# An LSTM with a binary FFN behind it: seven products for one block of 256 columns a quarter, and seven for two blocks of 512 a quarter

## Chip, cores and metric

The kernel runs on one core of a Trainium2 chip. The metric is the device time of one execution in microseconds (us); where several runs are given, it is their median.

## The reference

`x` is 32 sequences of 64 steps and 256 features. An LSTM with 256 units runs over it, and its hidden states go through a feed-forward network (FFN) of three layers whose weights are +1 or -1; the result is added to `x`.

```python
def step(carry, xw_t):                       # 64 steps, xW = x @ Wx + b
    prev_h, prev_c = carry
    a = xw_t + prev_h @ Wh                   # 32 x 1024
    i, f, o = sigmoid of the first three quarters of a
    g = jnp.tanh(a[:, 3 * Hd:])
    next_c = f * prev_c + i * g
    next_h = o * jnp.tanh(next_c)
    ...
h = jnp.concatenate([h, -h], axis=-1)        # all 2048 rows of hidden states
h = jax.nn.relu(s0 * _conn_dense(k0, h)) * 2     # 512 -> 1024
h = jax.nn.relu(s1 * _conn_dense(k1, h)) * 2     # 1024 -> 1024
h = s2 * _conn_dense(k2, h)                      # 1024 -> 256
return x + h
```

`_conn_dense` multiplies by a matrix that is 1.0 where its boolean kernel is true and -1.0 elsewhere.

## The kernel before

**Blocks.** The 64 steps are four blocks of 16 steps. A block gives the FFN 16 x 32 = 512 columns. In the FFN every activation is split into a high and a low part (`h` and `l`, fp32r tiles), and both are multiplied, so a product of one 128 x 128 piece of weights is two matmuls of 512 columns. Layer 0 of a block is 8 chunks of 4 matmuls (L594), the second layer ("layer 1", L620) 8 chunks of 16, layer 2 (L607) 32 matmuls: 192 in all (`ffn_block`). A chunk is evicted from PSUM by `evict` (L365): ScalarE writes relu to `h` (L368), VectorE writes the rest to `l` (L369).

**Steps.** A loop over the 64 steps issues, for each step: the products of h with Wh on TensorE (`gates_from_h`, L308: 32 matmul instructions in the trace), then the cell (`cell_step`): `sig`, `cand`, `sig` on ScalarE (L325 to L327), `kept`, `new` and `c` on VectorE (L329 to L333), `th` on ScalarE (L335), `h` and its transpose into `hist` on VectorE (L337, L342), and two ScalarE copies that put the next step's x part into the gate banks (L319, L320). Then comes a quota of other matmuls from a generator: products of x with Wx up to step 20 (`X_STEPS`, L63), FFN work from step 21 on. The quota is spread evenly:

```python
total_ffn = (NB - 1) * (4 * FC0 + 2 * FC0 * FC1 + 4 * FC1)
goal = (t + 1) * total_x // X_STEPS if t < X_STEPS else (t + 1 - X_STEPS) * total_ffn // (T - X_STEPS)
```

Here `total_ffn` is 576, three blocks. After the quota a step may issue one small chore: the split of four steps' h into `hhi` and `hlo` (`split_h`, L361, L362), a piece of weights, a sum of weight quarters (`make_sum`, L418), an output step (`output`, L372). The order of the program is kept on every engine (`manual_schedule`), so each engine has one queue and the matmuls of step t stand between the gates of t and those of t + 1.

**The last block** has its inputs only after the last step. `last_block` runs behind the loop. Its second layer is done in seven products instead of eight: weights and activations are cut into quarters (512 rows by 512 weights, and 512 rows by half of the block's columns, 256), and sums and differences of quarters are multiplied. The four tables of weight sums `s1` to `s4` are made in the steps, the sums and differences of activations (`differ`, `split`, L443, L449, L450) behind them, all on VectorE and ScalarE. A product is 32 matmuls of 256 columns (L459), so the seven are 224. Layer 2 (L564) is 64 matmuls of 256 columns, whose output has time as rows; `finish` scales it, adds x and stores it. The PSUM banks are four `pf`, two `po` and the two gate banks.

**Pools.** The x parts, the weight sums and the split quarters lie in `gpool` (28 buffers of 2 KB a partition), other activations in `apool` (24 buffers).

Of the kernel before, what the change touches and what calls it, by code (L numbers as in the profile page):

```python
# [43 lines left out]
def lstm_ffn(ctx: ExitStack, tc: tile.TileContext, x, cond, wx_d, wh_d, b_d, k0_d, k1_d, k2_d, s0_d, s1_d, s2_d, out):  # L44
# [29 lines left out]
    gpool = ctx.enter_context(tc.tile_pool(name="xg", bufs=28))  # L74
    apool = ctx.enter_context(tc.tile_pool(name="act", bufs=24))
# [28 lines left out]
    wh = const.tile([P, 2, G], F32, name="wh")  # L104
    wx = wpool.tile([P, 2, G], F32, tag="wx", name="wx")
    w0 = const.tile([P, 2, F0], F32R, name="w0")
# [154 lines left out]
    def evict_x(p, t):  # L261
        xg[t] = gpool.tile([P, 2, 4 * HQ], F32, tag="xg", name=f"xg{t}")
        b = bias.rearrange("p g j -> p (g j)").unsqueeze(1).to_broadcast([P, 2, 4 * HQ])
        load[0] += 1
        nc.vector.tensor_tensor(xg[t], p.rearrange("p t g j -> p t (g j)"), b, ALU.add)  # L265
# [132 lines left out]
    K2, F2, CB = FC0 // 2, F1 // 2, TB // 2  # L398
    sums = {}

    def make_sum(s, k):
# [3 lines left out]
        if s == 4:  # L405
            if k == 0:

                sums[s] = wpool.tile([P, K2, F2], F32R, tag="wx", name="s4")
            t = sums[s][:, k]
        else:  # L410
            t = gpool.tile([P, F2], F32R, tag="xg", name=f"s{s}_{k}")
# [9 lines left out]
    def parts(pool, tag, name):  # L421
        return [pool.tile([P, 2, CB], F32R, tag=tag, name=f"{name}{s}") for s in "hl"]

    def last_block(b):

        hi, lo = hparts.pop(b)
        full, b11, b2, t, a1 = [], {}, {}, {}, {}
        t2 = hpool.tile([P, K2, CB], F32, tag="hlo", name="t2")
        u = hpool.tile([P, 2, 2, CB], F32, tag="hhi", name="u")

        def quarter(i, k):

            return {1: full[k][:, 0], 2: t2[:, k], 3: full[k][:, 1], 4: full[K2 + k][:, 0]}[i]

        def differ(i, k):

            in0, in1 = {
                1: (full[k][:, 1], full[k][:, 0]),
                2: (full[K2 + k][:, 1], full[k][:, 0]),
                3: (full[K2 + k][:, 1], full[k][:, 1]),  # L440
                4: (full[K2 + k][:, 0], t2[:, k]),
            }[i]
            nc.vector.tensor_tensor(quarter(i, k), in0, in1, ALU.subtract)  # L443

        def split(i, k):
            if k % 2 == 0:
                t[i, k // 2] = parts(gpool, "xg", f"t{i}_{k}")
            h, l = (a[:, k % 2] for a in t[i, k // 2])
            nc.scalar.copy(h, quarter(i, k))  # L449
            nc.vector.tensor_tensor(l, quarter(i, k), h, ALU.subtract)  # L450

        def side(i):
            return lambda k, n: t[i, k // 2][n][:, k % 2]

        def product(bank, pair, a, b, first, last):
            for i in range(2):
                for k in range(K2):
                    for n in range(2):
                        nc.tensor.matmul(  # L459
                            bank[pair][:, i],  # L460
                            a(k)[:, ts(2 * pair + i, P)],
                            b(k, n),
                            start=first and i == 0 and k == 0 and n == 0,
                            stop=last and k == K2 - 1 and n == 1,
                            skip_group_check=True,
                        )

        def bank(name):
            return [ps_f.tile([P, 2, CB], F32, tag="pf", name=f"{name}{pair}") for pair in range(2)]

        def take(rows, half, pair, p):

            h, l = parts(apool, "act", f"c{rows}{half}_{pair}")
            nc.scalar.activation(h, p, AF.Relu)
            nc.vector.scalar_tensor_tensor(l, p, 0.0, h, ALU.max, ALU.subtract)
            for i in range(2):
                a1[rows * K2 + 2 * pair + i, half] = h[:, i], l[:, i]

        def take_sum(rows, half, pair, p, c):
            nc.vector.tensor_tensor(c, p, c, ALU.add)  # L480
            take(rows, half, pair, c)

        for m in range(FC0):
            p = ps_f.tile([P, TB], F32, tag="pf", name=f"p0_{b}_{m}")
            for n, (k, a) in enumerate(((0, hi), (0, lo), (1, hi), (1, lo))):
                nc.tensor.matmul(p, w0[:, k, ts(m, P)], a[:, k, :], start=(n == 0), stop=(n == 3))  # L486
            f = act([P, 2, CB], F32, f"f_{m}")
            full.append(f)
            nc.scalar.activation(f.rearrange("p c n -> p (c n)"), p, AF.Relu)
            if m < K2:  # L490
                if m % 2 == 0:
                    b11[m // 2] = parts(apool, "act", f"b11_{m}")
                h, l = (t[:, m % 2] for t in b11[m // 2])
                f = f[:, 0]
            else:
                b2[m - K2] = h, l = parts(apool, "act", f"b2_{m}")
            nc.scalar.copy(h, f)
            nc.vector.tensor_tensor(l, f, h, ALU.subtract)
            if m > K2:
                for i in (1, 2):  # L500
                    differ(i, m - K2 - 1)
            yield

        res = [xpool.tile([P, 2, D], F32, tag="x", name=f"res{half}") for half in range(2)]
        for i in range(NQ):
            nc.sync.dma_start(out=res[i // 2][:, i % 2], in_=x_in[:, ts(b * NQ + i, SH)])
        for i in (1, 2):
            differ(i, K2 - 1)


        x = bank("x")
        q = [g.rearrange("p (i n) -> p i n", i=2) for g in gate_banks]

        for pair in range(2):
            product(x, pair, lambda k: w1[:, k, :F2], lambda k, n: b11[k // 2][n][:, k % 2], True, False)
            nc.scalar.copy(q[pair], x[pair])
            for k in range(2):
                split(2, 2 * pair + k)
        for pair in range(2):
            product(x, pair, lambda k: w1[:, K2 + k, :F2], lambda k, n: b2[k][n][:, 0], False, True)  # L520
        for k in range(K2):
            split(1, k)
        for pair in range(2):
            take(0, 0, pair, x[pair])

        for pair in range(2):
            product(q, pair, lambda k: sums[2, k], side(2), False, False)
        nc.scalar.copy(u[:, 0], q[0])
        for i in (3, 4):
            for k in range(K2):  # L530
                differ(i, k)
            for k in range(K2):
                split(i, k)
            if i == 3:
                nc.scalar.copy(u[:, 1], q[1])

        v = [act([P, 2, CB], F32, f"v{pair}") for pair in range(2)]
        for pair in range(2):
            product(q, pair, lambda k: sums[1, k], side(1), False, False)
            nc.scalar.copy(v[pair], q[pair])  # L540

        r = bank("r")
        for pair in range(2):
            product(r, pair, lambda k: sums[3, k], side(3), True, False)
        for pair in range(2):
# [225 lines left out]
```

## Time and profile before

| what | value |
|---|---|
| median of 3 runs | 312.12 us (311.91 to 312.54) |
| span of the profiled execution, first to last instruction | 311.0 us |
| TensorE (PE) busy, granted clock | 304.9 us, 1.00 |
| VectorE (DVE) busy | 177.6 us |
| ScalarE (ACT) busy | 143.1 us |
| GpSimd (POOL) busy | 6.6 us |
| gates of step 21 start, gates of step 63 start | 80.8 us, 260.0 us |
| last matmul ends | 306.7 us |

The only time of its own that the profiled execution carries is its span; the runs' times also hold what lies before the first and behind the last instruction, and the median is 1.1 us above the span. Rows of the profile give start or group, engine, line of the kernel, operation, output and inputs, partitions x elements, and a count or mean duration. PEld is the loading of weights, which lies beside the matmuls. A matmul's duration overlaps with its neighbours', so what counts of it is the distance between two starts. "Idle before" names what ended an engine's wait.

### The profile page before, as it was taken

To read this page: it belongs to the slowest core of one execution; us is meant where nothing else is said; L and a number is where in the kernel's file an instruction comes from. 1 tells how busy PE (TensorE), PEld (TensorE's weight loads), DVE (VectorE), ACT (ScalarE), POOL (GpSimd) and SP (SyncE) were. 2 spreads that over 40 slices of the span, in tenths; PEclk is the share of its full clock that TensorE was granted. 3 is DMA by queue.
4 is the path that set the end of the run, shared out by engine and by line. 5 is a ranking of instruction groups with operands and counts; after the bars stand their busy time and mean duration, and the time that the engine had idled before them with its cause. 6 is when DMAs were issued, how large, how long until landed. Compare 5 with 4: busy or idle time off the path is not lost.

```text
span 311.0 us, 9795 instructions
## 1 busy us (share of the span) xinstructions
PE 304.9 (98%) x4138; PEld 242.4 (78%) x4138; DVE 177.6 (57%) x527; ACT 143.1 (46%) x512; POOL 6.6 (2%) x24
## 2 busy tenths in 40 slices
PE   7999999999999999999999999999999999999994
PEld 3888888787777777777777777777777777899994
DVE  2466767777673444455755444568564444599441
ACT  0224657774564543444633433356443333786320
POOL 5300000000000000000000000000000000000000
PEclk9999999999999999999999999999999999999999
DMA  6864001143000000000010000000410000031001
GB/s 186 210 185 108 6 10 49 36 93 67 3 2 0 2 2 0 3 2 0 2 38 14 22 1 2 2 2 6 98 34 2 3 0 2 25 80 32 2 0 68
DMA packets 27450, 10.88 MB, mean 35 GB/s; under 512 B 23560, under 2 KB 26632, under 8 KB 27408
## 3 DMA queue, kind: packets, MB, share of 16 engines
q1 hardware_dynamic: 24768, 8.66, 11.3%
q10 hardware_dynamic: 2400, 1.57, 1.8%
q8 instruction: 32, 0.52, 0.7%
q14 instruction: 10, 0.08, 0.1%
q0 software_dynamic: 240, 0.04, 0.1%
HBM read 8.16 MB, written 2.10 MB: 33 GB/s over the span
## 4 chain that ended last, share of the span: by engine, by line
PE 96%; DMA 1%; DVE 1%; SPq 0%; ACT 0%; issue 0%; ACTq 0%
PE p L620 30%; PE gates L308 20%; PE px L249 18%; PE p L594 8%; PE po L607 7%; PE gates L459 4%; PE r L459 2%; PE x L459 2%; PE po L564 2%; PE p L486 2%; DMA wx<-in_L_cond_Wx_dram 1%; SPq L96 0%; DVE a_7l L369 0%; DVE o L574 0%; PE p_bias L661 0%
## 5 line engine op out<-in xcount | busy, mean ns | idle before, releaser
L308 PEld LDWEIGHTS gates<-wh,hist 128*32 128x32 f32 x2016 | 54.6, 109 | 22.3 <-issue 13.4
L308 PE MATMUL gates<-wh,hist 128*32 128x192 f32 x2016 | 68.1, 275 | 0.0
L249 PE MATMUL px<-wx,xT 128*32 128x256 f32 (+1 forms) x1168 | 60.7, 355 | 0.4 <-DMA wx<-in_L_cond_Wx_dram 0.4
L325 ACT ACTIVATE sig<-gates 128x128 f32<-128x128 f32 x64 | 17.7, 277 | 79.8 <-PE gates L308 79.6
L249 PEld LDWEIGHTS px<-wx,xT 128*32 128x32 f32 x1168 | 42.2, 111 | 12.3 <-DVE xT L232 1.3
L329 DVE TENSOR_TENSOR kept<-sig,c 128x64 f32<-128x64 f32 x63 | 14.2, 225 | 49.1 <-ACT sig L325 48.8
L335 ACT ACTIVATE th<-c 128x64 f32<-128x64 f32 x64 | 16.4, 257 | 31.4 <-DVE c L333 31.4
L337 DVE TENSOR_TENSOR h<-sig,th 128x64 f32<-128x64 f32 x64 | 14.4, 225 | 20.7 <-ACT th L335 20.7
L265 DVE TENSOR_TENSOR xg<-px,bias 128x512 f32<-128x512 f32 x32 | 21.2, 670 | 2.8 <-PE px L249 2.3
L319 ACT COPY gates<-xg 128x192 f32<-128x192 f32 x64 | 20.0, 313 | 1.5 <-DVE xg L265 1.5
L594 PE MATMUL p<-hhi,w 128*128 128x512 f32 x48 | 19.3, 402 | 0.0
L594 PE MATMUL p<-hlo,w 128*128 128x512 f32 x48 | 19.1, 397 | 0.0
L342 DVE STREAM_TRANSPOSE hist<-h 128x64 f32<-128x64 f32 x64 | 15.7, 245 | 2.4
L333 DVE TENSOR_TENSOR c<-kept,new 128x64 f32<-128x64 f32 x64 | 14.4, 225 | 2.2
L327 ACT ACTIVATE sig<-gates 128x64 f32<-128x64 f32 x64 | 14.9, 233 | 0.1
L326 ACT ACTIVATE cand<-gates 128x64 f32<-128x64 f32 x64 | 14.0, 218 | 0.0
L331 DVE TENSOR_TENSOR new<-sig,cand 128x64 f32<-128x64 f32 x64 | 13.9, 217 | 0.0
L320 ACT COPY gates<-xg 128x64 f32<-128x64 f32 x64 | 13.0, 203 | 0.0
L594 PEld LDWEIGHTS p<-hhi,w 128*128 128x128 f32 x48 | 9.0, 188 | 2.1
L594 PEld LDWEIGHTS p<-hlo,w 128*128 128x128 f32 x48 | 9.0, 188 | 1.9
L214 ACT ACTIVATE w<-bits,nsgn,sgn 128x1024 fp32r<-128x1024 uint8 x8 | 9.9, 1240 | 0.0
L620 PE MATMUL p<-a_7h,w 128*128 128x512 f32 x24 | 9.9, 412 | 0.0
(250 smaller groups left out, 603.1 us busy)
## 6 DMA issues: line engine op xcount, KB each, us to landing
x<-in_x_dram SPq DMA_DIRECT2D x52, 64.0 KB, 2.7
out_dram<-o SPq DMA_DIRECT2D x28, 64.0 KB, 1.8
bits<-in_L_ffn_k_dram SPq DMA_DIRECT2D x10, 128.0 KB, 2.7
wx<-in_L_cond_Wx_dram SPq DMA_DIRECT2D x2, 256.0 KB, 4.8
wx<-in_L_cond_Wx_dram ACTq DMA_DIRECT2D x4, 128.0 KB, 5.1
wh<-in_L_cond_Wh_dram ACTq DMA_DIRECT2D x2, 256.0 KB, 5.3
wh<-in_L_cond_Wh_dram SPq DMA_DIRECT2D x2, 256.0 KB, 5.8
k<-in_L_ffn_k_dram SPq DMA_DIRECT2D x2, 256.0 KB, 3.1
```

What stands on the lines that cost most here:

```text
L249: nc.tensor.matmul(p[q * N : (q + 1) * N, t % 2, slots], xT[i // 2, i % 2][:, s, k, :], wx_q[:, k, q, slots], start=start, stop=False, ski ...
L265: nc.vector.tensor_tensor(xg[t], p.rearrange("p t g j -> p t (g j)"), b, ALU.add)
L308: nc.tensor.matmul(g[q * N : (q + 1) * N], hT[:, k, :], wh_q[:, k, q, slots], start=False, stop=(k == 1), skip_group_check=True,)
L319: nc.scalar.copy(gates[0], x_t[:, :3])
L325: nc.scalar.activation(sig[:, 0:2, :], gates[0][:, 1:3], AF.Sigmoid)
L327: nc.scalar.activation(sig[:, 2, :], gates[1][:, 0], AF.Sigmoid)
L335: nc.scalar.activation(th, c, AF.Tanh)
L342: nc.vector.transpose(hT, h.rearrange("p (j b) -> p b j", b=2))
L459: nc.tensor.matmul(bank[pair][:, i], a(k)[:, ts(2 * pair + i, P)], b(k, n), start=first and i == 0 and k == 0 and n == 0, stop=last and k ...
L594: nc.tensor.matmul(p, w0[:, k, ts(m, P)], a[:, k, :], start=(n == 0), stop=(n == 3))
L607: nc.tensor.matmul(po[m], w2[:, m, k], a1[k][n], start=(k == 0 and n == 0), stop=(k == FC1 - 1 and n == 1))
L620: nc.tensor.matmul(p1[m], w1[:, k, ts(m, P)], a0[k][n], start=(k == 0 and n == 0), stop=(k == FC0 - 1 and n == 1),)
```

## The change

The second layer of the last two blocks is done together in seven products. The two halves of the columns are now two whole blocks (512 columns each), so a product is 32 matmuls of 512 columns. The first two blocks stay as they were. Layer 0 of the block before last and the first of the seven products (`q[i]` with `a11`, copied to `p1`) are given out in the steps, the quota being 442 matmuls; layer 0 of the last block, the other six products and layer 2 of both blocks follow behind the last step. The evicted parts of the block before last are also added up again to a whole tile `f[m, 0]` on GpSimd (8 sums), and 8 of the differences of quarters behind the last step are made on GpSimd; the others are on VectorE. The first chunk of the next block's layer 0 is issued ahead of a block's last layer 2 matmuls. The two pools become one of 52 buffers. `wh` and `w0` move to a pool from which their room is given, once they have been read for the last time, to the split tiles `t1` and then `t4`. The residual loads and the store of the block before last move behind the last step. Lines that only moved or that are the replaced body of `last_block` are left out below.

```diff
-    gpool = ctx.enter_context(tc.tile_pool(name="xg", bufs=28))
-    apool = ctx.enter_context(tc.tile_pool(name="act", bufs=24))
+    apool = ctx.enter_context(tc.tile_pool(name="act", bufs=52))
...
-    wh = const.tile([P, 2, G], F32, name="wh")
+    wh = wpool.tile([P, 2, G], F32, tag="wh", name="wh")
     wx = wpool.tile([P, 2, G], F32, tag="wx", name="wx")
-    w0 = const.tile([P, 2, F0], F32R, name="w0")
+    w0 = wpool.tile([P, 2, F0], F32R, tag="w0", name="w0")
...
-        xg[t] = gpool.tile([P, 2, 4 * HQ], F32, tag="xg", name=f"xg{t}")
+        xg[t] = act([P, 2, 4 * HQ], F32, f"xg{t}")
...
-            t = gpool.tile([P, F2], F32R, tag="xg", name=f"s{s}_{k}")
+            t = act([P, F2], F32R, f"s{s}_{k}")
...
@@ -418,184 +417,206 @@
         nc.vector.tensor_tensor(t, in0, in1, op)
         sums[s, k] = t
-    def parts(pool, tag, name):
...
+    f, parts = {}, {"b11": {}, "b21": {}}
+    def layer0(p, m, hi, lo):
+        for n, (k, a) in enumerate(((0, hi), (0, lo), (1, hi), (1, lo))):
+            nc.tensor.matmul(p, w0[:, k, ts(m, P)], a[:, k, :], start=(n == 0), stop=(n == 3))
+            if n < 3:
+                yield 1
+    def first_chunk(b, m):
+        p = ps_f.tile([P, TB], F32, tag="pf", name=f"p0_{b}_{m}")
+        yield from layer0(p, m, *hparts[b])
+        f[m, 0] = act([P, TB], F32, f"f0_{m}")
+        h, l = evict(p, f"b{m}")
+        nc.gpsimd.tensor_tensor(f[m, 0], h, l, ALU.add)
+        parts["b11" if m < K2 else "b21"][m % K2] = h, l
+        yield 1
+    def last_blocks(b):
+        a1 = {}
+        def four_banks(name):
+            return [*gate_banks, *(ps_o.tile([P, TB], F32, tag="po", name=f"{name}{i}") for i in range(2))]
+        def product(bank, i, a, b, first, last):
+            for k in range(K2):
+                for n in range(2):
+                    nc.tensor.matmul(
+                        bank,
+                        a(k)[:, ts(i, P)],
+                        b[k][n],
+                        start=first and k == 0 and n == 0,
+                        stop=last and k == K2 - 1 and n == 1,
+                        skip_group_check=True,
+                    )
+                    if not (k == K2 - 1 and n == 1):
+                        yield 1
+        def differ(out, in0, in1, engine=nc.vector):
+            engine.tensor_tensor(out, in0, in1, ALU.subtract)
+        def pair(name):
+            return [act([P, TB], F32R, f"{name}{s}") for s in "hl"]
+        def split(a, h, l):
+            nc.scalar.copy(h, a)
+            differ(l, a, h)
+        def large(name):
+            both = [wpool.tile([P, K2, TB], F32R, tag=tag, name=f"{name}{tag}") for tag in ("wh", "w0")]
+            parts[name] = [[t[:, k] for t in both] for k in range(K2)]
+        def take(rows, half, i, p):
+            h, l = pair(f"c{rows}{half}_{i}")
             nc.scalar.activation(h, p, AF.Relu)
             nc.vector.scalar_tensor_tensor(l, p, 0.0, h, ALU.max, ALU.subtract)
-            for i in range(2):
...
+            a1[rows * K2 + i, half] = h, l
+        def take_sum(rows, half, i, p, c):
             nc.vector.tensor_tensor(c, p, c, ALU.add)
-            take(rows, half, pair, c)
-
+            take(rows, half, i, c)
+        a11, a12 = (lambda k: w1[:, k, :F2]), (lambda k: w1[:, K2 + k, :F2])
+        a22 = lambda k: w1[:, K2 + k, F2:]
+        for m in range(1, FC0):
+            yield from first_chunk(b, m)
+        del hparts[b]
+        q = [ps_f.tile([P, TB], F32, tag="pf", name=f"q{i}") for i in range(K2)]
+        p1 = [act([P, TB], F32, f"p1_{i}") for i in range(K2)]
+        for i in range(K2):
+            yield from product(q[i], i, a11, parts["b11"], True, False)
+            nc.scalar.copy(p1[i], q[i])
+            yield 1
+        hi, lo = hparts.pop(b + 1)
+        t2 = [hpool.tile([P, 2, TB], F32, tag=tag, name=f"t2{tag}") for tag in ("hhi", "hlo")]
+        t2 = [t2[k // 2][:, k % 2] for k in range(K2)]
+        parts["t2"] = {}
         for m in range(FC0):
-            p = ps_f.tile([P, TB], F32, tag="pf", name=f"p0_{b}_{m}")
...
+            if m % 4 == 0:
+                banks = four_banks(f"p0_{b + 1}_{m}_")
+            p = banks[m % 4]
+            yield from layer0(p, m, hi, lo)
+            f[m, 1] = act([P, TB], F32, f"f1_{m}")
+            nc.scalar.activation(f[m, 1], p, AF.Relu)
+            k = m % K2
             if m < K2:
-                if m % 2 == 0:
...
+                differ(f[k, 0], f[k, 1], f[k, 0])
             else:
-                b2[m - K2] = h, l = parts(apool, "act", f"b2_{m}")
...
+                differ(t2[k], f[m, 1], f[k, 0])
+                parts["t2"][k] = pair(f"t2_{k}")
+                split(t2[k], *parts["t2"][k])
+            yield 1
+        y = four_banks("y")
+        large("t1")
+        for i in range(K2):
+            yield from product(y[i], i, a12, parts["b21"], True, True)
+            split(f[i, 0], *parts["t1"][i])
+            differ(f[i, 1], f[K2 + i, 1], f[i, 1], nc.gpsimd)
+            yield 1
+        load_x(b, 0, [nc.sync])
+        load_x(b, 1, [nc.sync])
         res = [xpool.tile([P, 2, D], F32, tag="x", name=f"res{half}") for half in range(2)]
         for i in range(NQ):
-            nc.sync.dma_start(out=res[i // 2][:, i % 2], in_=x_in[:, ts(b * NQ + i, SH)])
...
+            nc.sync.dma_start(out=res[i // 2][:, i % 2], in_=x_in[:, ts((b + 1) * NQ + i, SH)])
+        u, v = {}, {}
+        for i in range(K2):
+            yield from product(q[i], i, lambda k: sums[2, k], parts["t2"], False, False)
+            differ(f[K2 + i, 0], f[K2 + i, 0], t2[i], nc.gpsimd)
+            take_sum(0, 0, i, y[i], p1[i])
+            u[i] = act([P, TB], F32, f"u{i}")
+            nc.scalar.copy(u[i], q[i])
+            yield 1
+        parts["t3"] = {}
         for k in range(K2):
-            split(1, k)
...
+            parts["t3"][k] = pair(f"t3_{k}")
+            split(f[k, 1], *parts["t3"][k])
+        parts["b22"] = {}
+        for k in range(K2):
+            parts["b22"][k] = pair(f"b22_{k}")
+            split(f[K2 + k, 1], *parts["b22"][k])
+        for i in range(K2):
+            yield from product(q[i], i, lambda k: sums[1, k], parts["t1"], False, False)
+            v[i] = act([P, TB], F32, f"v{i}")
+            nc.scalar.copy(v[i], q[i])
+            yield 1
+        r = four_banks("r")
+        large("t4")
+        for k in range(K2):
+            split(f[K2 + k, 0], *parts["t4"][k])
+        for i in range(K2):
+            yield from product(r[i], i, lambda k: sums[3, k], parts["t3"], True, False)
+            take_sum(1, 1, i, r[i], v[i])
+            yield 1
+        for i in range(K2):
+            yield from product(r[i], i, a22, parts["t4"], False, True)
+            take_sum(1, 0, i, r[i], u[i])
+            yield 1
+        for i in range(K2):
+            yield from product(q[i], i, lambda k: sums[4, k], parts["b22"], False, True)
+            take(0, 1, i, q[i])
+            yield 1
+        po = [ps_o.tile([P, TB], F32, tag="po", name=f"po{b}_{m}") for m in range(2)]
+        for m in range(2):
+            for k in range(FC0):
                 for n in range(2):
                     nc.tensor.matmul(
-                        po[i][:, :D].rearrange("p (q m j) -> p q m j", q=NQ, m=2),
-                        a1[k, half][n][:, ts(i % 2, P)],
+                        po[m], w2[:, m, k], a1[k, 0][n], start=(k == 0 and n == 0), stop=(k == FC0 - 1 and n == 1)
+                    )
+                    yield 1
+        for _ in output(b, po):
+            pass
+        pl = [ps_f.tile([P, TB], F32, tag="pf", name=f"po{b + 1}_{i}") for i in range(NQ)]
+        order = [*range(K2, FC0), *range(K2)]
+        for i in range(NQ):
+            for k in order:
+                for n in range(2):
+                    nc.tensor.matmul(
+                        pl[i][:, :D].rearrange("p (q m j) -> p q m j", q=NQ, m=2),
+                        a1[k, 1][n][:, ts(i, P)],
                         w2[:, :, k].rearrange("p m (q j) -> p q m j", q=NQ),
-                        start=k == order[half][0] and n == 0,
-                        stop=k == order[half][-1] and n == 1,
+                        start=k == order[0] and n == 0,
+                        stop=k == order[-1] and n == 1,
                     )
-
...
+            o = act([P, D], F32, f"o{b + 1}_{i}")
+            nc.vector.scalar_tensor_tensor(o, pl[i][:, :D], total, res[i // 2][:, i % 2], ALU.mult, ALU.add)
             for s, engine in enumerate((nc.sync, nc.scalar)):
-                engine.dma_start(out=out[ts(s, N // 2), ts(b * NQ + i, SH)], in_=o[ts(s, P // 2)])
...
+                engine.dma_start(out=out[ts(s, N // 2), ts((b + 1) * NQ + i, SH)], in_=o[ts(s, P // 2)])
+            yield 1
+    a0s = {}
+    def layer0_chunk(b, m):
+        if b == NB - 2:
+            yield from first_chunk(b, m)
+            return
+        p = ps_f.tile([P, TB], F32, tag="pf", name=f"p0_{b}_{m}")
+        yield from layer0(p, m, *hparts[b])
+        a0s[b, m] = evict(p, f"a0_{b}_{m}")
+        yield 1
     def ffn_block(b):
-        hi, lo = hparts.pop(b)
...
+        for m in range(min(b, 1), FC0):
+            yield from layer0_chunk(b, m)
+        a0 = [a0s.pop((b, m)) for m in range(FC0)]
+        del hparts[b]
         for half in range(2):
             load_x(b, half, [nc.sync])
         po = [ps_o.tile([P, TB], F32, tag="po", name=f"po{b}_{m}") for m in range(2)]
@@ -632,6 +653,7 @@
                 if m >= 2 and m < FC1 - 1:
                     yield from layer2([(0, m - 2), (1, m - 2)])
         last = FC1 - 1
+        yield from layer0_chunk(b + 1, 0)
         yield from layer2([(0, last - 2), (0, last - 1), (1, last - 2)])
         yield from layer2([(0, last), (1, last - 1), (1, last)])
         outputs.append(output(b, po))
@@ -686,9 +708,9 @@
     def ffn():
-        for b in range(NB - 1):
+        for b in range(NB - 2):
             yield from ffn_block(b)
-        yield from last_block(NB - 1)
+        yield from last_blocks(NB - 2)
     chores = deque()
@@ -700,7 +722,7 @@
     work = x_products(AHEAD, T)
     total_x = (T - AHEAD) * 4
-    total_ffn = (NB - 1) * (4 * FC0 + 2 * FC0 * FC1 + 4 * FC1)
+    total_ffn = (NB - 2) * (4 * FC0 + 2 * FC0 * FC1 + 4 * FC1) + 4 * FC0 + 4 * 2 * K2 - 6
     done = 0
     for t in range(T):
         load[0] = 0
```

## The prediction

> **What bounds the kernel now.** I read four views of the profile: the page's busy table and chain, then the instructions of one step in order of time, then the chain of waits, then the groups by line and shape for the price of one instruction.
>
> The page first:
>
> ```profile
> PE 304.9 (98%) x4138; PEld 242.4 (78%) x4138; DVE 177.6 (57%) x527; ACT 143.1 (46%) x512; POOL 6.6 (2%) x24
> PE 96%; DMA 1%; DVE 1%; SPq 0%; ACT 0%; issue 0%; ACTq 0%
> PEclk9999999999999999999999999999999999999999
> ```
>
> TensorE (PE) is busy 98% of the span and is 96% of the chain that ended last, at the full granted clock throughout. Vector (DVE) and scalar engine (ACT) are about half idle, GpSimd (POOL) ends its work in the first 12 us. So the time is the sum of PE's instructions, as long as nothing makes PE wait.
>
> Whether something could is read from one step (step 45) of the recurrence:
>
> ```profile
> 183.19 1.08 PE L308 MATMUL gates<-wh,hist 128*32 128x192 f32 x32
> 184.17 0.28 ACT L325 ACTIVATE sig<-gates 128x128 f32<-128x128 f32 x1 [2.08 <-PE gates L308]
> 184.48 0.23 DVE L329 TENSOR_TENSOR kept<-sig,c 128x64 f32<-128x64 f32 x1 [1.07 <-ACT sig L325]
> 184.88 0.22 DVE L333 TENSOR_TENSOR c<-kept,new 128x64 f32<-128x64 f32 x1
> 185.43 0.22 DVE L337 TENSOR_TENSOR h<-sig,th 128x64 f32<-128x64 f32 x1 [0.32 <-ACT th L335]
> 185.68 0.24 DVE L342 STREAM_TRANSPOSE hist<-h 128x64 f32<-128x64 f32 x1
> ...
> 187.37 1.08 PE L308 MATMUL gates<-wh,hist 128*32 128x192 f32 x32
> ```
>
> Columns: start, duration, engine, line. The new h is ready at 185.92, and the gates that need it start at 187.37, behind 13 FFN matmuls in PE's queue: 1.45 us to spare. A step with 13 matmuls takes 4.18 us, one with 14 takes 4.41 us (both lengths recur in the timeline), so a 512-column matmul costs 0.227 and a step without FFN work 1.23 us. In every step from 21 on the spare time is 0.79 to 1.67 us: the recurrence is never late.
>
> The end of the chain, in order of time (start, length, what, how many), prices the work behind the steps:
>
> ```profile
> 264.91 7.26 PE p L486 x32
> 272.17 7.67 PE x L459 x64
> 279.85 7.68 PE gates L459 x64
> 287.52 7.68 PE r L459 x64
> 295.20 3.84 PE gates L459 x32
> 299.05 7.63 PE po L564 x64
> ```
>
> These lie end to end: 7.26/32 = 0.227 for a matmul of 512 columns, 7.67/64 = 0.120 for one of 256. Two narrow ones cost 0.240, so a narrow product costs 6% more than a wide one. One wait of PE in this part is in the list of waits: `PEld po L607 <- DVE a_7l`, 0.5 us, once, before the last layer 2; by the timeline the matmul that should follow 262.98 at 263.21 starts at 263.49, so it costs 0.3.
>
> **The change, part by part.** *Matmuls.* Before, three blocks of 192 and one layer 0 of 32 make 608 matmuls of 512 columns; the last block adds 224 + 64 of 256. After: two blocks of 192, two layer 0 of 32, seven products of 32 (224), one layer 2 of 32: 704 of 512 columns, and the same 64 of 256. So 96 x 0.227 = +21.8 and 224 x 0.120 = -26.9: **-5.1 us**. The rest of PE (gates, x products) is as before.
>
> *Where they lie.* The steps' quota falls from 576 to 442 matmuls over 43 steps, from 13.4 to 10.3 a step; a step of 10 takes 1.23 + 2.27 = 3.50 us. That alone moves work, it removes none. The spare time for h falls by 3 x 0.227 = 0.68 to 1.45 - 0.68 = 0.77 us (1.0 with 11). The delays seen now are at most 0.66 (in step 50 the row of 0.68 us for s, L418, stands ahead of kept and leaves 0.79 of 1.45). They still fit: 0.
>
> *The gap at a block's end.* The first chunk of the next layer 0 is put between the last layer 1 and the last layer 2: four matmuls (0.9 us) cover the 0.3. -0.3.
>
> *Entry into the last layer 0.* After the gates of step 63 come 11 + 6 = 17 matmuls, 3.9 us. Its h is ready 1.66 us after the gates, but on ACT two copies of p1 (0.59 each, the second behind the ninth matmul) stand ahead of the cast of h (0.66 in the timeline), and DVE then needs 0.63: about 0.15 + 9 x 0.227 + 0.2 + 0.6 + 0.66 + 0.63 = 4.3 us. So 0.3 late: +0.3, which cancels the previous term. Bounds 0 and 1.0 (should ACT be a further op late).
>
> *Cover behind the last step.* PE has there 17 + 32 + 192 + 32 wide and 64 narrow matmuls, 69.6 us. DVE has some 52 ops of 0.67 to 0.69, four transposes of 0.42, two scalings of 0.74 and four of 0.48: about 41 us; ACT about 52 of 0.6: 31 us. The sums pass; the order is tighter. (a) For t2, each of four chunks goes relu 0.59, difference 0.67, copy 0.6 before ACT takes the next relu, some 2 us; the last piece is ready about 13.3 us after this layer 0 starts, PE asks for it after 32 + 32 matmuls, 14.5 us: 1.2 to spare, more where ops overlap. (b) The eight splits for t3 and b22 (4.8 us on each engine) run under a 7.3 us product. (c) In the take_sum rows DVE waits for ACT between its two ops: 0.69 + 0.6 + 0.69, 2 us against 1.8 of PE; over four products it falls 0.8 behind with about 2 in hand. PSUM banks are free earlier in each case. Cost 0, and if this cover is gone, what it lacks, up to 2 us.
>
> *Residuals and stores.* Four loads of x for the block before last move behind the steps, onto SP's queue ahead of four loads of res (3.4 us to landing); both are needed some 50 us later: 0. The end is the same four narrow groups, scaling and stores.
>
> *GpSimd.* Sixteen operations of 128x512 with both operands in SBUF are new there: eight sums f = h + l inside the steps (one at step 58, seven with 28 matmuls of layer 0, so over 28/10.3 = 2.7 steps), and eight differences behind the steps. The trace has no such operation: POOL's only TENSOR_TENSOR rows have one column.
>
> ```profile
> L184 POOL TENSOR_TENSOR total<-total,s 128x1 f32<-128x1 f32 x1 | 0.2, 189 | 0.1
> L418 DVE TENSOR_TENSOR s<-w,s 128x512 fp32r<-128x512 f32 x4 | 2.7, 681 | 0.0
> L329 DVE TENSOR_TENSOR kept<-sig,c 128x64 f32<-128x64 f32 x63 | 14.2, 225 | 49.1 <-ACT sig L325 48.8
> ```
>
> The same shape on DVE takes 0.68; I bound POOL's by that and by twice it, 1.36 (its two operands read one after the other), and take the middle, 1.0. Their results are wanted late (f by the last layer 0, the differences by t3 and t4 ten us after their inputs), so their own length is covered. What isn't bounded by any row is whether DVE runs undisturbed beside them. Lower bound 0. Upper bound: a two-operand DVE instruction waits until the sum on POOL has ended. The sums start when a chunk's l is written, and DVE writes l after the transpose of a step, just ahead of the next kept; so two or three of them, back to back, lie over kept, c and h, and behind a waiting kept stand new, c, h and the transpose, for which ACT (th) and then PE (gates) wait. Of 2.6 sums a step I let two stand in the chain (one ahead of kept, one between two of its links): 2 x 1.0 - 0.77 = 1.2 us a step, three steps: **+3.7 us**. With 0.68 a sum it is 3 x 0.6 = 1.8, with 1.36 it is 3 x 1.95 = 5.9. The differences behind the steps meet (a) and (c), which can absorb one each; I take 0 there, at most 1.5.
>
> I take the upper bound of the mechanism, since the sums are released exactly where the chain's two-operand rows stand and there are 2.6 of them a step: a share of waiting already uses the 0.77.
>
> The Trainium skill, in the page "SBUF — State Buffer", section "Who interferes with whom", speaks against the change: a DVE instruction with two SBUF inputs and a GpSimd instruction that reads SBUF exclude each other, and the second to issue waits for the whole of the first. No run here shows it yet. Under that rule the sum is the one with waits, without it the one of 307.0. "GPSIMD Engine Reference", section "Performance versus the Vector engine", has 4497 ns for an add of 2048 columns; a quarter, 1.12 us, is an estimate from it and would make the step term 3 x (2.24 - 0.77) = 4.4 and the time 311.4.
>
> *Sum.* In the profiled execution 311.0 - 5.1 - 0.3 + 0.3 + 3.7 = 309.6 us of span; the median of the runs, 312.1, lies 1.1 above that span and I keep this distance: **310.7 us**.
>
> **The rivals.** *Free GpSimd.* The sums disturb nobody and the step keeps its 0.77 of spare time: 312.1 - 5.1 = **307.0** (306.5 to 308). For it: DVE is only about half busy, and nothing in the profile shows the two engines in each other's way. Against: nothing shows them side by side at all.
>
> *GpSimd holds the recurrence, slower than before.* Place: the three steps of layer 0 of the block before last. Price: at 1.36 a sum and with all 2.6 of them in the chain, 3 x (3.5 - 0.77) = 8.2 us, so 312.1 - 5.1 + 8.2 = **315.2**. It decides from 5.1 us of waits on, which is 5.1/3 + 0.77 = 2.5 us of held time a step, two sums of 1.24. That is inside my bounds for the sum, so this is no remote case.
>
> **How the numbers follow.** My forecast, two sums held a step, 0.52; it spans 308.8 (0.68 a sum) to 312.9 (1.36), and up to 314 with the tail's 1.5. Free GpSimd 0.29; held throughout 0.19. About 0.2% (0.6 us) is what a measurement of this kernel can tell from no change, so faster means under 311.5: 0.32 of my 0.52 and 0.28 of the free case, 0.60. Same is 0.12 of mine and a rest, 0.13. Slower is 0.08 of mine and the whole third case, 0.27. The range for 8 in 10 takes in the free case, and the third case almost to its price: 306.4 to 315.0. My own case alone would have 308.8 to 314.
>
> **What would show it.** Right: steps 22 to 57 of 3.5 to 3.75 us with PE unbroken; then three steps longer by one to two us, in which kept, c or h start late behind a POOL row of the sums, and gates wait for hist; behind the steps products of 32 matmuls in 7.26 us end to end. The free case shows 3.5 us in steps 58 to 62 too. Wrong: gaps of PE before t2's, t4's or b22's products, or periods over 3.75 us in steps without sums; or sums on POOL far outside 0.68 to 1.36.

## The result, and the profile after

The changed kernel is slower: 318.05 us in the median of 4 runs (317.53 to 318.18) against 312.12; the ratio is 1.0185, with a 95% interval of 1.017 to 1.0199. I had forecast 310.7, with 306.4 to 315.0 for 8 in 10, and put 0.27 on slower. The profiled execution has a span of 316.1 us.

The same rows of the page, busy time first, then two engines over the 40 slices:

```profile
PE 301.8 (95%) x4010; PEld 233.6 (74%) x4010; DVE 198.9 (63%) x523; ACT 147.2 (47%) x514; POOL 30.0 (9%) x40
...
PE   7999999999999999999999999999679988999994
...
POOL 5200000000000000000000000003630581000000
```

PE is busy 3.1 us less, and not the 5.1 that the count of matmuls gave; the kernel e12 below, which has the same matmuls and almost no gaps, is busy 299.6 us, 5.3 less. PE is no longer unbroken: behind the first slice, its six, seven and eights all stand in slices in which POOL has work. Step 61 of the timeline, in the same columns as step 45 in the prediction:

```profile
226.02 0.68 DVE L368 SCALAR_TENSOR_TENSOR b5l<-p,b5h 128x512 fp32r<-128x512 f32 x1
226.15 0.28 ACT L324 ACTIVATE sig<-gates 128x128 f32<-128x128 f32 x1 [0.28 <-PE gates L307]
226.19 1.29 POOL L434 TENSOR_TENSOR f<-b4h,b4l 128x512 f32<-128x512 f32 x1 [2.32 <-DVE b4l L368]
226.62 0.93 DVE L328 TENSOR_TENSOR kept<-sig,c 128x64 f32<-128x64 f32 x1
227.43 1.29 POOL L434 TENSOR_TENSOR f<-b5h,b5l 128x512 f32<-128x512 f32 x1
227.48 1.33 DVE L330 TENSOR_TENSOR new<-sig,cand 128x64 f32<-128x64 f32 x1
228.84 0.22 DVE L332 TENSOR_TENSOR c<-kept,new 128x64 f32<-128x64 f32 x1
...
229.65 0.24 DVE L341 STREAM_TRANSPOSE hist<-h 128x64 f32<-128x64 f32 x1
...
230.04 1.08 PE L307 MATMUL gates<-wh,hist 128*32 128x192 f32 x32 [1.29 <-DVE hist L341]
```

`kept` and `new` took 0.22 us each in the kernel before. Here `kept` is issued while POOL adds `b4` and ends just behind it; then POOL's second sum gets in ahead of `new`, which ends just behind that. `c` starts 2.69 us behind the start of `sig` instead of 0.71, 2.0 us late, and PE waits for `hist`. The row of `b5l`, whose first input is in PSUM, lies for 0.51 us of its length beside the same sum and keeps its 0.68. Steps 58, 60, 61 and 62 take 3.73, 5.85, 4.86 and 5.02 us; by their matmuls they should take 3.50, 3.73, 3.50, 3.50. That is 5.2 us. Steps 22 to 57 take 3.50 or 3.73 us (one 3.55).

The rest is lost behind the steps. First the timeline while t2 is made:

```profile
247.88 1.78 DVE L460 TENSOR_TENSOR t2hhi<-f,f 128x512 f32<-128x512 f32 x1
...
250.88 1.30 POOL L460 TENSOR_TENSOR f<-f,f 128x512 f32<-128x512 f32 x1 [1.78 <-ACT f L510]
250.95 1.78 DVE L460 TENSOR_TENSOR t2hlo<-f,f 128x512 f32<-128x512 f32 x1
252.77 0.62 ACT L466 CAST t_2h<-t2hlo 128x512 fp32r<-128x512 f32 x1 [1.97 <-DVE t2hlo L460]
253.29 0.59 ACT L510 ACTIVATE f<-p 128x512 f32<-128x512 f32 x1
...
253.94 0.50 PE L448 MATMUL y<-b4h,w 128*128 128x512 f32 x1 [0.89 <-ACT f L510]
...
255.23 3.45 POOL L460 TENSOR_TENSOR f<-f,t2hhi 128x512 f32<-128x512 f32 x2
...
257.45 5.78 DVE L460 TENSOR_TENSOR t1w<-f,t1wh 128x512 fp32r<-128x512 f32 x4
```

A difference of 0.69 us becomes 1.78 behind POOL's difference; the cast waits for it, the next relu stands behind the cast, and PE needs the bank that this relu reads. The four rows of `t1w` further down take 5.78 us together, three of them 1.77 or 1.78 each, and the first `take_sum` stands behind them in VectorE's queue. Then the list of waits, for all four products with `s1`, and the end of the chain:

```profile
PEld q L448 <- ACT u L538: 3.0, 4, 1.9
```

```profile
274.82 0.52 ACT b_3h L466
275.34 1.94 ACT v L552 x4
277.28 0.53 ACT t4wh L466
...
277.83 2.50 DVE t4w L460 x4
280.33 0.61 DVE v L481
281.08 4.07 PE gates L448 x16
285.14 4.10 PE r L448 x16
289.24 7.25 PE q L448 x32
296.50 7.25 PE po L579 x32
303.75 7.63 PE po L591 x64
```

The chain that ended last now runs over DVE and ACT until 281.08; two groups of 16 matmuls take 4.1 us instead of 3.63 (16 x 0.227), the rest is end to end as forecast. I add up, behind the gates of step 63, by how much the distance of two matmul starts exceeds 0.227 us (512 columns) or 0.120 (256): 5.3 us, against 0.5 in the kernel before. Which of the small excesses are counted moves such a sum by 0.1 to 0.2. By product it is 1.4 us at `y` and the product with t2 behind it, 2.4 at `q` with t1, 1.3 at the products with t4, and 0.3 elsewhere.

The account of the spans: matmuls -5.1, steps 58 to 62 +5.2, waits behind the steps +4.8, and 4.7 in place of 4.3 us from the last matmul to the end, +0.4. The changed kernel's step 21 also started 0.55 us earlier (over all profiles here it starts between 79.96 and 81.12, with no connection to the edits). Together +4.8; measured 5.1, of which 0.3 stays unassigned. The medians are 5.9 apart; for the kernel before, later executions have spans of 310.4 to 310.6 at 312.2 to 312.4 us, so its profiled one was on the long side.

### The profile page after: what moved, and what is told of

Read it like the earlier page. It is cut to its first block, busy times and chain, and to the rows that moved or that the text cites. A ratio compares the mean times of both kernels' runs of the same rounds, so it can differ in the third digit from the quotient of the medians.

```text
span 316.1 us, 9587 instructions
## 1 busy us (share of the span) xinstructions
PE 301.8 (95%) x4010; PEld 233.6 (74%) x4010; DVE 198.9 (63%) x523; ACT 147.2 (47%) x514; POOL 30.0 (9%) x40
## 5 line engine op out<-in xcount | busy, mean ns | idle before, releaser
L328 DVE TENSOR_TENSOR kept<-sig,c 128x64 f32<-128x64 f32 x63 | 17.6, 279 | 38.5 <-ACT sig L324 38.1
L424 PE MATMUL p<-hhi,w 128*128 128x512 f32 x56 | 22.6, 403 | 0.0
L424 PE MATMUL p<-hlo,w 128*128 128x512 f32 x56 | 22.2, 397 | 0.0
L434 POOL TENSOR_TENSOR f<-b0h,b0l 128x512 f32<-128x512 f32 x1 | 1.3, 1288 | 201.6 <-DVE b0l L368 201.6
L330 DVE TENSOR_TENSOR new<-sig,cand 128x64 f32<-128x64 f32 x64 | 17.3, 270 | 0.0
L424 PEld LDWEIGHTS p<-hhi,w 128*128 128x128 f32 x56 | 10.5, 188 | 2.5
L424 PEld LDWEIGHTS p<-hlo,w 128*128 128x128 f32 x56 | 10.5, 188 | 2.3
```

The source lines that it names most:

```text
L328: nc.vector.tensor_mul(kept, sig[:, 1, :], c)
L330: nc.vector.tensor_mul(new, sig[:, 0, :], cand)
```

## The experiments

My theory was that a VectorE row with two SBUF operands waits for a whole GpSimd operation, and that this causes the waits in the steps and part of those behind them; the expectations call it the port theory. Rivals: GpSimd's results are merely late; VectorE and ScalarE are late by themselves. "Steps" is what steps 58 to 62 lose, "behind" the sum of excess distances as above, both from the profile in us; time and ratio from the runs.

| kernel | steps | behind | median us | ratio to before (95%) |
|---|---|---|---|---|
| the change | 5.2 | 5.3 | 318.05 | 1.0185 (1.017 to 1.0199) |
| e1 step sums on VectorE | 4.1 | 5.0 | 316.38 | 1.0143 (1.0102 to 1.0184) |
| e2 differences on VectorE | 5.2 | 2.9 | 315.21 | 1.0092 (1.0073 to 1.011) |
| e3 both | 4.1 | 2.7 | 314.27 | 1.0061 (1.0042 to 1.0079) |
| e4 no sums, differences on VectorE | 0 | 2.8 | 310.13 | 0.9924 (0.9903 to 0.9944) |
| e5 sums behind the transpose | 1.3 | 4.0 | 315.00 | 1.0086 (1.0062 to 1.0111) |
| e6 and tail reordered | 1.3 | 2.0 | 312.64 | 1.0008 (0.9991 to 1.0025) |
| e7 memset for the sum | 0 | 2.9 | 310.47 | 0.9935 (0.9917 to 0.9953) |
| e8 copy for the sum | 0.3 | 2.9 | 310.85 | 0.9947 (0.9929 to 0.9964) |
| e9 as e6, no new tile | 1.3 | 2.3 | 310.88 | 0.9950 (0.9938 to 0.9962) |
| e10 half of the sums later | 0 | 3.4 | 310.32 | 0.9935 (0.9922 to 0.9948) |
| e11 pad in the kernel before | | | 315.32 | 1.0106 (1.0084 to 1.0129) |
| e12 no sums, tail reordered | 0 | 0.8 | 307.80 | 0.9854 (0.9842 to 0.9867) |
| e13 sums in the gaps of t2 | 0 | 0.9 | 308.30 | 0.9868 (0.9847 to 0.9889) |

**The two groups of GpSimd work, each alone (e1 to e4).**

```diff
-        nc.gpsimd.tensor_tensor(f[m, 0], h, l, ALU.add)
+        nc.vector.tensor_tensor(f[m, 0], h, l, ALU.add)                 # e1, e3
...
-            differ(f[i, 1], f[K2 + i, 1], f[i, 1], nc.gpsimd)
+            differ(f[i, 1], f[K2 + i, 1], f[i, 1])                      # e2, e3, e4
...
-            differ(f[K2 + i, 0], f[K2 + i, 0], t2[i], nc.gpsimd)
+            differ(f[K2 + i, 0], f[K2 + i, 0], t2[i])                   # e2, e3, e4
...
-        f[m, 0] = act([P, TB], F32, f"f0_{m}")
...
+        f[m, 0] = h                                                     # e4, no sum
```

e1: 

> The eight sums f = h + l in the steps are made on VectorE instead of GpSimd; the eight differences behind the steps stay on GpSimd. Port theory (a two-operand VectorE row waits for the whole GpSimd sum): the waits in kept and new of 0.7 to 1.1 us go, but each sum now takes some 0.6 us of VectorE's own queue ahead of the next kept, two or three a step against 0.77 to spare, so steps 58 to 62 lose 1.5 to 4 us instead of 5.2, the part behind the steps keeps its 4.8 of waits: 314.5 to 317. Rival (GpSimd's work is merely long and late, nobody waits for a port): nothing in the recurrence needs these sums, so VectorE gets more work and no wait goes: 318 or more.

e2: 

> The eight differences behind the steps are made on VectorE; the sums in the steps stay on GpSimd. Port theory: steps 58 to 62 keep their 5.2 us of waits; behind the steps the 1.8 us rows of t2 and the 1.4 us rows of t1 fall back to 0.7, so that of the 4.8 us of waits at y, q and r at most 2 remain: 315 to 316. Rival (VectorE and ScalarE take turns behind the steps and are late by themselves): 4.8 us of waits or more remain, since VectorE has eight rows of 0.68 more: 318 to 321.

e3: 

> Both edits: all sixteen on VectorE, nothing of this kind on GpSimd. Port theory: the two gains add, 318.0 - 2.5 - 2.5, 311 to 314, and no VectorE row of 64 columns is longer than 0.3 us. Rival (late vector and scalar work): 318 or more.

e4: 

> The eight sums in the steps are left out (the high part h stands for f, so the low part is missing from the differences), the differences are on VectorE. This is the change's matmul work without GpSimd and without the sums. Port theory: steps of 3.50 or 3.73 us up to the last, 5.1 us less matmul time than the kernel before, at most 2 us of waits behind the steps: 307 to 309. If the matmul count were not worth 5.1 us, the steps would be as short and the time still near 312.

Moving the differences takes 2.8 us off the time and 2.4 off the waits behind the steps; e2's steps stay as they were. Moving the sums gives 1.7 us, at the upper end of what I expected: on VectorE a sum takes 0.69 us, starts when its own `l` is complete, and stands ahead of `kept` and of the split of h. By the times alone e1 isn't clear of the change (one of its four runs took 318.86, and the two intervals overlap); its trace is, since no row of `kept` or `new` is longer than 0.26 us, where seven were 0.93 to 1.33. In e3 the two gains add up in the steps and behind them; in the medians it is 3.8 us of 2.8 + 1.7, and at 314.27 e3 is 0.3 over my range. The rivals that wanted 318 or more for e2 and e3 are out by their times. Without the sums (e4) the steps lose nothing; the sums therefore cost 5.2 us on GpSimd and 4.1 on VectorE where they are issued. But e4 missed my 307 to 309: 2.8 us of waits remain with nothing on GpSimd at all.

**What it is in a GpSimd operation that holds VectorE (e7, e8).** Both leave the sums out like e4, and put one of these in the place of the sum:

```diff
+        spare = act([P, TB], F32, f"spare{m}")
+        nc.gpsimd.tensor_copy(spare[:, :1], l[:, :1])      # e7
+        nc.gpsimd.memset(spare, 0.0)                       # e7
...
+        nc.gpsimd.tensor_copy(spare, l)                    # e8
```

e7: 

> The sums are left out as in the fourth experiment (h stands for f); in their place GpSimd reads one column of l and then fills a 128x512 tile with zero, the result unused. It works at the same moments but hardly reads SBUF. Port theory (it is the reading of SBUF by GpSimd that excludes a two-operand VectorE row): kept and new stay at 0.23 us, time as in the fourth experiment, 309.5 to 311. Rival (any GpSimd work on SBUF beside VectorE holds it up): waits of up to the fill's length, 312 to 315.

e8: 

> The same with a copy of l (128x512, one operand read) in place of the sum, the result unused. Port theory: it reads SBUF, so kept and new wait for it for its whole length; if a copy is about half as long as a sum, two of them take 1.3 us a step of which 0.77 is spare: 311 to 313; if it is as long, 314 to 316. Rival (only a GpSimd instruction with two operands holds VectorE up): as the fourth experiment, 309.5 to 311.

The timeline of the memset kernel in step 60, then of the copy kernel in the same step:

```profile
221.06 0.21 DVE L328 TENSOR_TENSOR kept<-sig,c 128x64 f32<-128x64 f32 x1
221.19 0.21 DVE L330 TENSOR_TENSOR new<-sig,cand 128x64 f32<-128x64 f32 x1
221.24 0.53 POOL L436 MEMSET spare<- 128x512 f32 x1
221.44 0.23 DVE L332 TENSOR_TENSOR c<-kept,new 128x64 f32<-128x64 f32 x1
```

```profile
220.19 0.70 DVE L361 TENSOR_TENSOR hlo<-hist,hhi 128x256 fp32r<-128x256 f32 x1
220.41 0.97 POOL L435 COPY spare<-b3l 128x512 f32<-128x512 f32 x1
220.81 0.64 DVE L328 TENSOR_TENSOR kept<-sig,c 128x64 f32<-128x64 f32 x1
```

`c`, with both operands in SBUF, runs in its 0.23 us right through a memset of 0.53. The copy, which reads one operand, first waits for `hlo` (0.97 us instead of the 0.61 of a copy that nothing disturbs) and then holds `kept` (0.64 instead of 0.22). So it is GpSimd's reading that excludes a two-operand VectorE row, both ways; a second operand is not needed. e8's steps lose only 0.3 us, less than I expected, since at 0.61 us a copy fits into what the step has to spare. Its time, 310.85, lies in the range of its rival too, so it is these rows that decide against the rival, and not the time.

**When the sums are issued, and the order behind the steps (e5, e6, e9).** The sums wait behind a one-column copy that reads the transposed h; in e6 and e9 also `u` is copied ahead of `take_sum`, and b22 is split behind the `take_sum` of r:

```diff
+    pending = deque()
+    gate = const.tile([P, 1], F32, name="gate")            # e5, e6
+    gate = warm[:, 36:37]                                  # e9
...
+    def late_sums(behind, most):
+        if pending:
+            nc.gpsimd.tensor_copy(gate, behind)
+        for _ in range(min(most, len(pending))):
+            o, h, l = pending.popleft()
+            nc.gpsimd.tensor_tensor(o, h, l, ALU.add)
...
         c, hT = cell_step(t, c)
+        if t < T - 1:
+            late_sums(hT[:, 0, :1], 2)
...
+    late_sums(hparts[NB - 1][1][:, 0, :1].bitcast(F32), 8)
...
-            take_sum(0, 0, i, y[i], p1[i])                 # e6, e9
             u[i] = act([P, TB], F32, f"u{i}")
             nc.scalar.copy(u[i], q[i])
+            take_sum(0, 0, i, y[i], p1[i])                 # e6, e9
```

e5: 

> All eight sums are on GpSimd again, but at most two a step, and each pair stands behind a one-column copy that reads the transposed h of its step; the differences are on VectorE. Only the moment of the sums differs from the second experiment. Port theory: a pair of 1.3 us each starts when the step's last two-operand row is done and has some 2 us until the next kept, so kept is up to 0.8 us late against 0.77 to spare: steps 58 to 62 lose at most 1 us in all instead of 5.2, 310 to 311.7. Rival (the sums cost wherever they stand, by their number or length): 314 to 316, as in the second experiment.

e6: 

> As the one with sums behind the transpose, and behind the steps two things change their place in the queues: the copy of q to u stands ahead of take_sum of y, and the splits of b22 stand behind the take_sums of r. The theory for the last 2.8 us of waits (q waits for u, which ScalarE does after a relu that waits for VectorE; r waits for v sums that stand behind t4 and so behind b22 on both engines): they fall to 1 us or less, 307.5 to 310. Rival (ScalarE and VectorE have too much work there in any order): no gain, 310 to 312.

e9: 

> As the kernel with sums behind the transpose and the reordered tail, but the column that GpSimd copies to lies in a spare column of an existing tile instead of a new 4-byte tile. In that kernel matmuls of 512 columns started 233 ns apart in place of 229. Theory (the new tile shifted the tiles laid out behind it by 4 bytes): the distance returns to 229 ns, some 700 matmuls x 4 ns = 2.8 us less, 309.3 to 310.5. Rival (the one-column copies themselves, or the order, cost it): 312.6 again.

The steps lose 1.3 us instead of 5.2 (I had at most 1), with the same sums on the same engine: place in time decides. e5 nevertheless came out at 315.0, 3 us over my expectation. Of that, 1.3 us is the entry into the last layer 0: the last two sums, of `b6` and `b7`, hold `new` and `c` of step 63 (1.31 and 1.33 us), and with them the split of h. Another part had nothing to do with the sums: `gate` was a new constant tile of 4 bytes a partition, and 512-column matmuls of the second layer started 233.3 ns apart instead of 229.4. In e9 the column lies in an existing tile; the distance is back at 229.4 and the time 1.8 us lower than e6's; I had expected 2.8. The reordering took 2.4 us (e5 to e6). e6 missed its 307.5 to 310 (312.64) and e9 its 309.3 to 310.5 (310.88): both keep the 1.3 us in the steps and the 1.3 at the entry.

**The 4 bytes by themselves (e11).**

```diff
+    pad = const.tile([P, 1], F32, name="pad")
+    nc.vector.memset(pad, 0.0)
```

> The kernel before, with one more unused constant tile of 4 bytes a partition behind warm, and nothing else. Theory of the 4-byte shift: 512-column matmuls some 4 ns longer where their operands moved, up to 608 x 4 ns = 2.4 us: 313.5 to 315. Rival (it was not the layout): 312.2, no change.

3.0 us slower, from an unused tile and the instruction that fills it, and 0.3 over my range. The clock doesn't account for it: granted 0.997 against 1.000 in the two profiled executions, an estimate of 0.7 ns of the 4.8 by which the distance of 512-column matmuls grew. The end of the chain of this kernel beside the same line of the kernel before (7.26 us for 32):

```profile
267.01 7.47 PE p L488 x32
```

**The order behind the steps without any sums (e12), and the sums put where they fit (e10, e13).** e10 keeps four sums on GpSimd, one a step behind the transpose, and makes the other four on VectorE with the splits of t1; e13 moves these four:

```diff
-                parts["t2"][k] = pair(f"t2_{k}")
-                split(t2[k], *parts["t2"][k])
+                parts["t2"][k] = th, tl = pair(f"t2_{k}")  # e13
+                nc.scalar.copy(th, t2[k])                  # e13
+                f[m, 0] = act([P, TB], F32, f"f0_{m}")
+                nc.vector.tensor_tensor(f[m, 0], *parts["b21"][k], ALU.add)
+                differ(tl, t2[k], th)
```

e12: 

> The fourth experiment (no sums, h stands for f, differences on VectorE) with the two changes of order behind the steps. Its 2.8 us of waits there fall under 0.8 if they came from the order of ScalarE's and VectorE's queues: 307.3 to 308.5, the 5.1 us of matmul time in full. If they came from the amount of their work, 309.5 to 310.5 as before.

e10: 

> As the one before, but only the four sums that the last layer 0 needs are on GpSimd in the steps, one a step behind the transpose; the other four are made on VectorE behind the steps, between the splits of t1. Port theory: one sum of 1.3 us fits into the 2 us between two chains, so steps of 3.50 and 3.73 us throughout, and the entry into the last layer 0 no longer waits for GpSimd (it lost 1.3 us): another 2 to 2.6 us less, 307 to 308.5, which is faster than both kernels. Rival (VectorE behind the steps can't take four more rows of 0.68): those come back as waits at q, 309.5 or more.

e13: 

> As the tenth experiment, but the four later sums stand on VectorE elsewhere: inside the chunks of t2, between the difference and the low part, where VectorE waits some 0.7 us for ScalarE's cast. Same instructions, same engines. Theory (place decides: in the tenth they delayed the splits of t1 and with them the relu, u and q): the 3.4 us of waits behind the steps fall to about 1, 307.8 to 309. Rival (VectorE has too much work behind the steps, wherever it stands): 310 or more.

In e4 a round of `take_sum` takes 2.6 us, and the copy of q to `u` stands behind its relu:

```profile
258.65 0.69 DVE L459 TENSOR_TENSOR b6h<-b6h,t2hlo 128x512 fp32r<-128x512 f32 x1
259.25 0.69 DVE L480 TENSOR_TENSOR p<-y,p 128x512 f32<-128x512 f32 x1
259.98 0.63 ACT L475 ACTIVATE c_2h<-p 128x512 fp32r<-128x512 f32 x1 [1.49 <-DVE p L480]
260.51 0.57 ACT L537 COPY u<-q 128x512 f32<-128x512 f32 x1
...
261.85 0.68 DVE L480 TENSOR_TENSOR p<-y,p 128x512 f32<-128x512 f32 x1
```

e12 takes the waits behind the steps from 2.8 to 0.8 us with the same instructions as e4. e10 has unbroken steps but missed 308.5: its four VectorE rows pushed the take_sums back, and 3.4 us of waits came at q and r. e13 has the same rows inside the 0.7 us in which VectorE waits for a cast:

```profile
240.69 0.69 DVE L471 TENSOR_TENSOR t2hhi<-f,f 128x512 f32<-128x512 f32 x1
241.30 0.68 DVE L530 TENSOR_TENSOR f<-b4h,b4l 128x512 f32<-128x512 f32 x1
241.42 0.62 ACT L528 CAST t_0h<-t2hhi 128x512 fp32r<-128x512 f32 x1 [0.76 <-DVE t2hhi L471]
242.07 0.69 DVE L471 TENSOR_TENSOR t_0l<-t2hhi,t_0h 128x512 fp32r<-128x512 f32 x1
```

The low part starts as soon as the cast is done, and the end of the chain is PE almost alone:

```profile
242.74 3.63 PE gates L459 x16
246.37 3.63 PE y L459 x16
250.00 14.51 PE q L459 x64
264.50 4.31 PE gates L459 x16
```

At 308.30 us it is the fastest complete version, ahead of both kernels: 0.9868 of the kernel before.

## Why the prediction was wrong

**Right.** Matmuls: e12, without sums and with 0.8 us of waits, runs in 307.8 us; I had 307.0 for the change without waits. Step length: 3.50 and 3.73 us as worked out. The mechanism in the steps, two sums held in the chain in each of three steps, is what the trace shows in steps 60 to 62 (step 58 adds one, 0.23 us). The rule of the Trainium skill that I had weighed against the change ("SBUF — State Buffer", section "Who interferes with whom") agrees with the traces: 0.93 and 1.33 us for rows of 0.22 beside GpSimd sums, 0.23 beside a memset (e7).

**Mis-sized.** A GpSimd sum takes 1.29 us; I took 1.0, from between 0.68 and 1.36. My own formula with 1.29 gives 3 x (2 x 1.29 - 0.77) = 5.4 against 5.2 measured. So 1.5 us of the miss is this term. The estimate of 1.12 us, a quarter of the 4497 ns for 2048 columns in the Trainium skill, "GPSIMD Engine Reference", section "Performance versus the Vector engine", was nearer, and still short. With 1.29 the sum of the prediction would have been 312.4, no gain. The term for the end of the program, put at nothing, was 0.4: the stores of the block before last fill SP's queue until 310.5 us, less than 1 us before the last matmul ends, and the last store goes out there 0.8 us behind its twin on ACT's queue. The 1.1 us that I kept between span and median came from one execution with a long span; here it is 2.0 (318.05 against 316.1), 0.9 of the miss.

**The step that failed** is "Cover behind the last step ... Cost 0", with the 0 that I took for the eight differences ("at most 1.5"). It cost 4.8 us. The sentence in it that "PSUM banks are free earlier in each case" is the one that the waits contradict: PE waited for the relu that reads the bank wanted by `y`, for the copies of q to `u`, and for the sum with `v` that reads the bank of r. Two things were wrong behind it. First, the differences on GpSimd hold VectorE there just as the sums do: (a) had 1.2 us in hand, while one held row costs 1.1 and there were three in a row; and the held rows of t1 put off the first `take_sum` to 263.15 us, whose rounds then take 2.05 us, as I had them. With the differences on VectorE (e2) the wait at `y` is gone and that at `q` falls from 2.4 to 1.5: 2.4 us in all. Second, (c) counted an engine's own alternation but not who stands behind it in the queues: the copy of q to `u`, which frees PE's bank, is behind the relu of a round of `take_sum` (2.6 us long in e2 and e4, as the difference stands in it too), and the first sum with `v` is behind t4, which stands behind b22, though b22 is wanted last. These are the other 2.4 us (e2's 2.9 less the 0.5 of the kernel before). That the order makes them is shown by e4 and e12, which differ in it alone: 2.8 against 0.8. The new order was not run with the differences on GpSimd.

My rival for the slower side had the right sign for another reason: it wanted every sum of a step in the chain (8.2 us), where two were, and the rest came from behind the steps.

What stays open: 0.3 us of the account; why 4 bytes cost 4 to 5 ns a matmul; and by what rule the waiting GpSimd operation goes ahead of a VectorE row that is queued.

## What to carry to other kernels

Work given to an idle GpSimd isn't free where VectorE works on two SBUF operands on the path that sets the end: price it by its own length for every such row that can be queued behind it (here up to 1.3 us for `kept` and as much again for `new`), and look at the moment it is released. The same eight sums cost 5.2 us in the steps released by their data. Held back until the step's last two-operand row was done they cost 1.3 us there at two a step, and 1.3 more at the entry into the last layer 0; four of them, at one a step, cost nothing. A sum of busy time that fits says little; follow each queue in order and ask what stands ahead of the one row that frees PE's bank.

## What was not expected of the hardware

An unused 4-byte tile laid out ahead of others made 512-column matmuls 4.8 ns longer each (228.5 to 233.3 ns between starts in the second layer of the kernel before, 3.0 us in all), while those of 256 columns got 1.5 ns shorter (120.0 to 118.5). GpSimd's waiting instruction went ahead of a VectorE row that was queued behind another: `kept` and `new` are issued 0.14 us apart when nothing disturbs them, and yet a whole sum of 1.29 us ran between them. And the start behind the first matmul after a wait is 0.34 us away instead of 0.227; it is as far behind the gates of every step, where PE hadn't waited, so no wait is needed for it.
